# Splitting the slot copies of the first stage over two engines, and new places and queues in the tail of a two-layer convolution kernel

## The chip, the cores and the metric

The kernel runs on one core of a Trainium2 chip. The core has a matrix engine (PE), a vector engine (DVE), an activation engine (ACT), GpSimd (POOL) and a queue engine (SP), which share 16 DMA engines. The metric is the device time of one launch in microseconds (us). The kernel before took 1919.48 us, the median of three runs (1914.35, 1919.48, 1921.25).

## What is computed

The input `x` is an image of 512 x 512 positions with 64 channels in float32, 64 MiB. Two layers follow each other, each of the form `x = x + layer(group_norm(x))`, with 32 groups of two channels normalised over the whole image.

```python
def _L0_conv_ref(x, ...):
    xn = _ln(x, norm_w, norm_b)
    left, right = xn @ left_w + left_b, xn @ right_w + right_b
    m = sequence_mask.astype(xn.dtype)
    mask = (m[:, :, None] * m[:, None, :])[..., None]
    left  = left  * mask * sigmoid(xn @ lgate_w + lgate_b)
    right = right * mask * sigmoid(xn @ rgate_w + rgate_b)
    out = einsum('bkjd,bkid->bijd', left, right)
    out = _ln(out, onorm_w, onorm_b) @ out_w + out_b
    return out * sigmoid(xn @ ogate_w + ogate_b)

def _L1_conv_ref(x, w_real, w_imag):      # keeps 12 x 12 Fourier modes
    x_ft = fft2(x)[..., :12, :12]
    out_ft = einsum('bcmn,comn->bomn', x_ft, w_real + 1j * w_imag)
    return real(ifft2(zero_pad(out_ft)))
```

The mask zeroes the rows and columns whose mask bit is 0. The kernel uses that only about half of the rows and columns count.

## The kernel before

A branch at the end of the program takes `compact` when at most 256 rows (`K`) have a mask bit. The trace shows that this branch runs. It works in stages.

**First stage (lines 642 to 674).** Each row of the image has a rank, with the masked-in rows first. The image is cut into 16 column blocks (`NJ`) of 32 columns (`JC`). Four gathers per block (`gather`, POOL's indirect DMAs of 1 MiB) bring rows in the order of rank, 128 rows each: `r = 0, 1` go into the two halves of an `xg` tile, `r = 2, 3` into two `yg` tiles. PE transposes each quarter into PSUM (`x_ps`, line 664), and DVE takes mean and variance from there (`bn_stats`, line 665, 16 per block; every fourth block `join_chunks` joins them; after block 8 `make_weights` prepares the projection weights). Of `xg`, which holds the masked-in rows, every column is also copied into the big tile `xc`, at a slot that is read from memory: `slots_of` loads ranks into registers, 16 per load (line 634), and line 669 issues one ACT copy of 128 x 128 numbers for each of the 32 columns. A masked-out column goes to a dummy slot, so several copies can have the same target. `xg` has 3 buffers, `yg` has 2. The order of the work on each queue is the order of the program (`manual_schedule`): on POOL the four gathers of a block, on ACT two register loads and 32 copies per block. When the stage is over, `group_norm_affine` forms the affine of the norm, and the next stage transposes `xc` (line 690) and scales it on ACT (line 692).

**Middle stages (lines 677 to 839).** Projections and gates, the products over the rows for each of 64 channels, and their results in the tile `places`, 128 partitions with eight places of 64 x 64 numbers each. The change doesn't touch these stages.

**Output stage (lines 841 to 1116).** A software pipeline over steps `s`, eight to a unit, 32 units of 64 positions x 128 rows. A unit is gathered again from `x`, normalised and gated; `gated` multiplies (line 962) and `added` adds to x (line 966) in quarters (`c`), both on POOL, except the last quarter of the last unit, which `engine_of` sends to DVE. `store` writes the new image to `x1_h` from SP's queue, `transform` (line 982) multiplies a unit into the Fourier sums, `save` copies them to the tile `f_t` (pool `of`, two buffers) and writes them to `modes_d`, `statistics` (line 1000) takes the statistics for the second group norm on DVE, and `fetch(h)` reads modes back to `modes_t`, a part of place 7. `fetch(3)`, the last, is issued on ACT's queue.

**Tail (lines 1118 to 1245).** The pools `lx` (three tiles) and `lq` (all small tiles of the second layer) take the memory of the closed pools of the output stage, in this order. POOL clears `picks` (line 1135), `fetch(3)` follows, then POOL gathers the first 13 (`AHEAD`) row blocks of 1 MiB ahead into free parts of `places` and the `lx` tiles. PE and DVE meanwhile end the group norm, mix the modes (line 1167) and transform back. Then for each of 64 row blocks PE makes the correction (`l_ps`, line 1229), DVE adds it to the gathered x (line 1236), SP stores the result, and POOL gathers a block 13 ahead.

Of the kernel before, what the change touches and what calls it, by code (L numbers as in the profile page):

```python
# [17 lines left out]
P = 128  # L18
# [12 lines left out]
NJ = N // JC  # L31
K = 2 * P
AHEAD = 13
QB = 4


# [9 lines left out]
def conv_preact_kernel(ctx: ExitStack, tc: tile.TileContext, t: dict):  # L46
# [89 lines left out]
    def load_weights(pool, queue):  # L136


        def per_channel(name):
            v = pool.tile([P, 1], F32, name="v_" + name)  # L140
            for r in range(2):
                queue.dma_start(v[r * C : (r + 1) * C, :], t[name].rearrange("(c o) -> c o", o=1))
            return v

        norms = {name: (per_channel(name + "_w"), per_channel(name + "_b")) for name in ("norm", "onorm")}
        loaded = []

        for name, norm, parts, split in (
            ("sides", "norm", ("left", "right"), True),
            ("gates", "norm", ("lgate", "rgate"), True),  # L150
            ("ogate", "norm", ("ogate", "ogate"), False),
            ("out", "onorm", ("out", "out"), False),
        ):
            raw = pool.tile([P, P], F32, name="raw_" + name)
            b = pool.tile([P, 1], F32, name="v_" + name)
            if not split:
                nc.vector.memset(raw, 0.0)
            for r in range(2):
                for k in range(2):
                    if split or r == k:  # L160
                        queue.dma_start(raw[r * C : (r + 1) * C, k * C : (k + 1) * C], t[parts[k] + "_w"])
                queue.dma_start(b[r * C : (r + 1) * C, :], t[parts[r] + "_b"].rearrange("(c o) -> c o", o=1))
            loaded.append((name, *norms[norm], raw, b, C if split else P))

        def make(keep):

            with tc.tile_pool(name="wps", bufs=2, space=PSUM) as wps:
                for name, nw, nb, raw, b, k in loaded:
                    scaled = pool.tile([P, P], F32, name="scaled_" + name, tag="scaled")
                    nc.vector.tensor_scalar(scaled, raw, nw, None, ALU.mult)  # L170
                    ps = wps.tile([P, P + 1], F32, name="ps_" + name, tag="ps")
                    nc.tensor.matmul(ps[:, :P], center, scaled, start=True, stop=True)
                    nc.tensor.matmul(ps[:, P : P + 1], raw[:k], nb[:k], start=True, stop=True)
                    weights[name] = keep.tile([P, P], F32, name="w_" + name)
                    biases[name] = keep.tile([P, 1], F32, name="b_" + name)
                    nc.vector.tensor_copy(weights[name], ps[:, :P])
                    nc.vector.tensor_add(biases[name], ps[:, P : P + 1], b)

        return make
# [430 lines left out]
    def compact(fc):  # L610
# [14 lines left out]
        def gather(dst, src, idx, r, jc):  # L625
            nc.gpsimd.indirect_dma_start(  # L626
                out=dst, out_offset=None, in_=src, in_offset=bass.IndirectOffsetOnAxis(ap=idx[:, r, jc : jc + 1], axis=0)
            )

        def slots_of(engine, jc):  # L630

            regs = []
            for k in range(0, JC, 16):
                _, some = nc.values_load_multi_w_load_instructions(
                    slot_row[0:1, jc * JC + k : jc * JC + k + 16], engines=(engine,), min_val=0, max_val=K,
                    skip_runtime_bounds_check_because="a rank is not negative, and the minimum with K was taken",
                )
                regs += some
            return regs


        with tc.tile_pool(name="xc", bufs=1) as cp:
            xc = cp.tile([P, K + 1, 2, C], F32, name="xc")
            with tc.tile_pool(name="f1", bufs=1) as sp, tc.tile_pool(name="f1x", bufs=3) as xp, tc.tile_pool(
                name="f1y", bufs=2
            ) as yp, tc.tile_pool(name="f1p", bufs=6, space=PSUM) as pt, tc.manual_schedule():
                make_weights = load_weights(sp, nc.sync)
                sets = chunk_sets(fc, 4, 1)
                quarter = NJ // 4
                for jc in range(NJ):  # L650
                    if jc % quarter == 0:
                        stats = sp.tile([P, 1, 16 * quarter, 6], F32, name="stats1c")
                    xg = xp.tile([P, 2, JC, C], F32, name="xg")
                    of_row = [xg[:, 0], xg[:, 1]] + [yp.tile([P, JC, C], F32, name="yg") for _ in range(2)]
                    for r in range(4):
                        gather(of_row[r].rearrange("p j c -> p (j c)"), tiles, src_i, r, jc)
                    for r in range(4):
                        flat = of_row[r].rearrange("p j c -> p (j c)")
                        for c in range(4):

                            ps = pt.tile([P, 4, P], F32, name="x_ps")
                            for i in range(4):
                                o = (8 * c + 2 * i) * C
                                nc.tensor.transpose(ps[:, i, :], flat[:, o : o + P], ident)  # L664
                            nc.vector.bn_stats(  # L665
                                stats[:, 0, 16 * (jc % quarter) + 4 * r + c, :], ps.rearrange("p i k -> p (i k)")
                            )
                    for j, slot in enumerate(slots_of(mybir.EngineType.Activation, jc)):
                        nc.scalar.copy(xc[:, bass.ds(slot, 1)].rearrange("p o r c -> p (o r) c"), xg[:, :, j, :])  # L669
                    if jc % quarter == quarter - 1:  # L670
                        join_chunks(sp, sets, jc // quarter, stats)
                    if jc == NJ // 2:
                        make_weights(fc)
                ab1 = group_norm_affine(fc, sets, 2 * stats.shape[2], "xc")


# [113 lines left out]
        with tc.tile_pool(name="tri", bufs=1) as trp:  # L790
# [54 lines left out]

            units = [(jc, half) for jc in range(NJ) for half in ((1, 0) if jc < NJ - 1 else (0, 1))]
            total_g = (first + len(units)) * SIZE
            with tc.manual_schedule(), tc.tile_pool(name="late", bufs=1) as lp, tc.tile_pool(name="of", bufs=2) as fp:
                sets = chunk_sets(lp, 8)
                col_basis = lp.tile([P, 4, M2], F32, name="col_basis")  # L850
                nc.scalar.dma_start(col_basis, t["c_table"][:, :, 2:])
# [22 lines left out]

                def fetch(h):

                    (nc.scalar if h == 3 else nc.sync).dma_start(modes_t, modes_d[h * P : (h + 1) * P])

                with tc.tile_pool(name="np_x", bufs=LEAD + 2) as tp, tc.tile_pool(name="np_q", bufs=2) as sqp, tc.tile_pool(
                    name="np_s", bufs=3  # L880
# [67 lines left out]
                        for j, slot in enumerate(slots_of(mybir.EngineType.SP, jc)):  # L948
                            nc.sync.dma_start(us[jc][:, j], u_d[:, bass.ds(slot, 1)].rearrange("p o r c -> p (o r) c"))


                    def engine_of(k, c):
                        return nc.vector if (k, c) == (len(units) - 1, 3) else nc.gpsimd

                    def gated(k, c):

                        jc, half = units[k]
                        if half == 0:
                            u = us[jc][:, 16 * (c % 2) : 16 * (c % 2) + 16, c // 2, :]
                        else:  # L960
                            u = rows_of["out"].unsqueeze(1).to_broadcast([P, 16, C])
                        engine_of(k, c).tensor_mul(zs[k, c], zs[k, c], u)  # L962

                    def added(k, c):
                        xr = x_of(k)[:, 16 * c : 16 * c + 16, :]
                        engine_of(k, c).tensor_add(xr, xr, zs.pop((k, c)))  # L966

                    def store(k, r):
                        jc, half = units[k]
# [16 lines left out]
                            )  # L986

                    def save(jc):
                        ft = fp.tile([P, 8, C], F32, name="f_t")
                        nc.scalar.copy(ft.rearrange("p j c -> p (j c)"), fs.pop(jc))  # L990
                        for g in range(4):
                            o = jc * JC + 8 * g
                            queue = nc.scalar if jc == NJ - 1 else nc.sync
                            queue.dma_start(modes_d[o : o + 8].rearrange("j m c -> m j c"), ft[32 * g : 32 * g + M2])
# [29 lines left out]
                    for s in range(-LEAD, total_g + 2 * SIZE):  # L1024
# [3 lines left out]
                        def held(i):  # L1028
                            return 0 <= v - i < len(units)
# [24 lines left out]

                        if n % 2 == 1:
                            i, c = (0, (n - 3) // 2) if n >= 3 else (1, 3)
                            if held(i):
                                gated(v - i, c)
                        else:
                            i, c = (0, (n - 4) // 2) if n >= 4 else (1, 2 + n // 2)  # L1060
                            if held(i):
                                added(v - i, c)
                        if 0 <= v + 3 < len(units):
                            if n == 3:
# [50 lines left out]
                            for part, name in enumerate(("w_real", "w_imag")):  # L1115
                                nc.sync.dma_start(wide[part * C : (part + 1) * C], t[name].rearrange("c o m n -> c o (m n)"))

                with tc.tile_pool(name="lx", bufs=1) as xp, tc.tile_pool(name="lq", bufs=1) as qp:

                    free = 3 * 64 * C + C * MODES * MODES  # L1120
                    buffers = [places[:, free : free + JC * C].rearrange("p (n c) -> p n c", c=C)]
# [195 lines left out]
```

## Time and profile before

| what | us |
|---|---|
| median of the runs | 1919.48 |
| profiled execution, its own time | 1910.37 |
| its span | 1908.6 |
| first stage, first gather to first transpose of the next stage | 14.40 to 226.11 |
| output stage and join, up to the last bn_stats of line 1000 | to 1574.57 |
| tail, first gather ahead to the end of the span | 1582.18 to 1908.6 |

The mean granted clock of the matrix engine is 0.892 of full speed. Over the whole span PE is busy 88%, DVE 77%, ACT 51%, POOL 43%. These shares are averages over stages with different limits, so the slices and windows of a stage say more than the totals: the row of digits in the page has 40 slices of 47.7 us, of which the first five hold the first stage and the last seven the tail. A group's row gives line, engine, operation, output and input with shapes, count, busy time and mean of one in ns, and then the idle time of the engine just before those instructions with what ended it. An engine's idle time matters only where something waits for it.

### The profile page before, as it was taken

Reading aid. Unit: us, or ns where it says so; the run is one execution under the profiler, and the core shown is the slowest. Engines: PE = TensorE matmul, PEld = TensorE weight load, DVE = VectorE, ACT = ScalarE, POOL = GpSimd, SP = SyncE. Lnnn points to the kernel's source line nnn. Section 1 sums busy time; section 2 is a strip of 40 time slices with the busy share of each in tenths; the row PEclk is TensorE's granted clock in tenths of the full one; section 3 lists DMA queues with packets and bytes.
Section 4 is the critical chain, followed back from the end, with each engine's and each line's share of the span. In section 5 each row is a group of like instructions: output and inputs, shape, how many; then the busy total and the mean of one; then the engine's idle time right before and its main releaser. Section 6 shows DMA issues by size and latency. Waiting matters only on the chain. (4 is left out here: it accounts for less than half of the span.)

```text
span 1908.6 us, 33697 instructions
## 1 busy us (share of the span) xinstructions
PE 1672.8 (88%) x11598; PEld 1351.7 (71%) x11598; DVE 1462.3 (77%) x2995; ACT 971.5 (51%) x1766; POOL 825.9 (43%) x517
## 2 busy tenths in 40 slices
PE   6776499999899999999999899999999966987873
PEld 5666466665677889998888888888888835654431
DVE  6988477777455558888999799989999994764552
ACT  3777766564222254567777577767777720111000
POOL 2322011111000000019999799979998973111110
PEclk9998799999899999999999899999999986555555
DMA  7988235556655534236876576767777579999999
GB/s 266 415 334 332 85 100 138 139 136 153 205 177 177 177 128 160 120 120 238 277 250 240 213 246 229 249 224 242 267 259 252 199 218 360 404 427 427 426 427 380
DMA packets 188867, 468.21 MB, mean 245 GB/s; under 512 B 35184, under 2 KB 134384, under 8 KB 147600
## 3 DMA queue, kind: packets, MB, share of 16 engines
q1 hardware_dynamic: 158192, 262.40, 40.6%
q0 software_dynamic: 27712, 201.40, 27.4%
q10 hardware_dynamic: 2784, 2.16, 0.4%
q8 instruction: 94, 1.54, 0.3%
q14 instruction: 85, 0.70, 0.1%
HBM read 278.13 MB, written 187.76 MB: 244 GB/s over the span
## 5 line engine op out<-in xcount | busy, mean ns | idle before, releaser
L918 PE MATMUL w_ps<-gate_x,xt_c 128*128 128x128 f32 x2048 | 283.3, 282 | 31.5 <-DVE z_t L1087 30.0
L966 POOL TENSOR_TENSOR places<-places,z_t 128x1024 f32<-128x1024 f32 x127 | 301.7, 2376 | 8.2
L918 PEld LDWEIGHTS w_ps<-gate_x,xt_c 128*128 128x128 f32 x2048 | 254.4, 195 | 48.1 <-DVE z_t L1087 48.0
L918 PE MATMUL c_ps<-center_x,xt_c 128*128 128x128 f32 x2048 | 277.2, 279 | 0.0
L918 PEld LDWEIGHTS c_ps<-center_x,xt_c 128*128 128x128 f32 x2048 | 253.6, 195 | 2.2 <-ACT xt_c L913 1.8
L928 ACT ACTIVATE sq_c<-c_ps 128x512 f32<-128x512 f32 x320 | 188.8, 590 | 104.1 <-PE c_ps L918 103.7
L1229 PE MATMUL l_ps<-places,rinv 24*128 24x512 f32 x512 | 209.9, 1098 | 35.5 <-DVE places L1236 29.4
L1087 DVE TENSOR_TENSOR z_t<-w_ps,rs_n 128x512 f32<-128x512 f32 x320 | 216.7, 677 | 23.3 <-PE w_ps L918 22.9
L1000 DVE BATCH_NORM_STATS2 stats2c<-places 128x6 f32<-128x128 f32 x1024 | 220.8, 280 | 8.4 <-POOL places L966 8.4
L1045 ACT ACTIVATE z_t<-z_t 128x1024 f32<-128x1024 f32 x128 | 135.6, 1060 | 141.8 <-DVE z_t L1090 136.9
L932 DVE TENSOR_REDUCE scratch<-sq_c 128x16 f32<-128x1024 f32 x160 | 194.8, 1218 | 16.9 <-ACT sq_c L928 12.2
L1229 PEld LDWEIGHTS l_ps<-places,rinv 24*128 24x128 f32 x512 | 118.5, 296 | 121.6 <-DVE places L1236 80.0
L1090 DVE TENSOR_TENSOR z_t<-z_t,scratch 128x1024 f32<-128x1024 f32 x160 | 195.4, 1221 | 11.8 <-ACT rs_n L938 3.5
L962 POOL TENSOR_TENSOR z_t<-z_t,bias_row_out 128x1024 f32<-128x1024 f32 x63 | 149.7, 2376 | 113.0 <-DMA places<-u_d 108.7
L908 PE MATMUL t_ps<-c_ident,places 128*128 128x128 f32 x1280 | 197.0, 277 | 1.3 <-DVE places L837 1.3
L1236 DVE TENSOR_TENSOR places<-places,l_ps 128x512 f32<-128x512 f32 x200 | 125.0, 683 | 90.0 <-DMA places<-x_h,dst_i 60.6
L913 ACT ACTIVATE xt_c<-t_ps,ab_xc 128x512 f32<-128x512 f32 x256 | 175.9, 687 | 23.4 <-PE t_ps L908 23.3
L908 PEld LDWEIGHTS t_ps<-c_ident,places 128*128 128x128 f32 x1280 | 149.3, 143 | 51.7 <-issue 50.8
L626 POOL DMA_INDIRECT places<-in_x,src_i x64 | 62.8, 981 | 264.4 <-PE c_ps L918 213.1
L669 ACT COPY xc<-xg 128x128 f32 x512 | 153.3, 299 | 46.2 <-issue 30.5
L665 DVE BATCH_NORM_STATS2 stats1c<-x_ps 128x6 f32<-128x512 f32 x256 | 157.4, 690 | 14.3 <-PE x_ps L664 13.6
L962 POOL TENSOR_TENSOR z_t<-z_t,places 128x1024 f32<-128x1024 f32 x64 | 151.7, 2370 | 31.2 <-ACT z_t L1045 30.1
(201 smaller groups left out, 2551.8 us busy)
## 6 DMA issues: line engine op xcount, KB each, us to landing
x_h<-places SPq DMA_DIRECT2D x64, 1024.0 KB
out_x<-places SPq DMA_DIRECT2D x50, 1024.0 KB
places<-u_d SPq DMA_DIRECT2D x512, 64.0 KB
left_d<-o_c SPq DMA_DIRECT2D x64, 256.0 KB
right_d<-o_c SPq DMA_DIRECT2D x64, 256.0 KB
left_raw<-left_d SPq DMA_DIRECT2D x64, 256.0 KB
right_raw<-right_d SPq DMA_DIRECT2D x64, 256.0 KB
u_d<-z_t SPq DMA_DIRECT2D x32, 512.0 KB
```

What stands on the lines that cost most here:

```text
L665: nc.vector.bn_stats(stats[:, 0, 16 * (jc % quarter) + 4 * r + c, :], ps.rearrange("p i k -> p (i k)"))
L908: nc.tensor.transpose(tps[:, i, :], flat[:, o : o + P], ident)
L913: nc.scalar.activation(xts[s], tps, AF.Identity, bias=ab1[:, 2:3])
L918: nc.tensor.matmul(ps[:, 2 * i : 2 * i + 2, :], xts[s][:, i, :], w, start=True, stop=True)
L928: nc.scalar.activation(sqs[s // 2][:, 8 * (n % 2) : 8 * (n % 2) + 8, :], cps, AF.Square)
L932: nc.vector.tensor_reduce(totals[k % 2][:, 8 * (n - 1) : 8 * (n + 1)], sqs.pop(s // 2), AX.X, ALU.add)
L962: engine_of(k, c).tensor_mul(zs[k, c], zs[k, c], u)
L966: engine_of(k, c).tensor_add(xr, xr, zs.pop((k, c)))
L1000: nc.vector.bn_stats(st[k // 4][:, g, k % 4, :], x_of(k)[:, :, 2 * g : 2 * g + 2])
L1087: nc.vector.tensor_mul(z[:, 8 * odd : 8 * odd + 8, :], wps, rs)
L1090: nc.vector.tensor_add(z, z, bias.unsqueeze(1).to_broadcast([P, 16, C]))
L1229: nc.tensor.matmul(ps.rearrange("p j o -> p (j o)"), rinv[h, b, :], it[h], start=True, stop=True, tile_position=(32 * g, 0),)
```

## The change

There are two parts. In the first stage, `slots_of` takes a range of columns. A new helper `keep` issues the copies of a range on a given engine: columns 0 to 21 (`SHARE`) on ACT, 22 to 31 on POOL. Gathers are issued by a new helper `fetch_tile`, two blocks at the start and then block `jc + 2` after the copies of block `jc`; `xg` has 2 buffers, `yg` has 4. Two weight tiles are allocated in the pool of `xc`.

In the tail, the pool `of` is gone and `save` uses a part of place 7. `fetch(3)` is issued on POOL's queue. The last quarter of the last unit is done by `finished` on DVE, in two halves through two PSUM tiles, where the bias also lies in PSUM, and the add follows at once instead of one step later. The pools `lq` and `lx` are opened in the other order.

```diff
+SHARE = 22
...
-        def slots_of(engine, jc):
+        def slots_of(engine, jc, first=0, last=JC):
...
-            with tc.tile_pool(name="f1", bufs=1) as sp, tc.tile_pool(name="f1x", bufs=3) as xp, tc.tile_pool(
-                name="f1y", bufs=2
+            with tc.tile_pool(name="f1", bufs=1) as sp, tc.tile_pool(name="f1x", bufs=2) as xp, tc.tile_pool(
+                name="f1y", bufs=4
...
+                def fetch_tile(jc):
+                    xg = xp.tile([P, 2, JC, C], F32, name="xg")
+                    xgs[jc] = xg, [xg[:, 0], xg[:, 1]] + [yp.tile([P, JC, C], F32, name="yg") for _ in range(2)]
+                    for r, part in enumerate(xgs[jc][1]):
+                        gather(part.rearrange("p j c -> p (j c)"), tiles, src_i, r, jc)
+
+                def keep(engine, copy, jc, first, last):
+
+                    for j, slot in enumerate(slots_of(engine, jc, first, last), first):
+                        copy(xc[:, bass.ds(slot, 1)].rearrange("p o r c -> p (o r) c"), xgs[jc][0][:, :, j, :])
+
+                fetch_tile(0)
+                fetch_tile(1)
...
-                    for j, slot in enumerate(slots_of(mybir.EngineType.Activation, jc)):
-                        nc.scalar.copy(xc[:, bass.ds(slot, 1)].rearrange("p o r c -> p (o r) c"), xg[:, :, j, :])
+                    keep(mybir.EngineType.Activation, nc.scalar.copy, jc, 0, SHARE)
+                    keep(mybir.EngineType.Pool, nc.gpsimd.tensor_copy, jc, SHARE, JC)
+                    del xgs[jc]
+                    if jc + 2 < NJ:
+                        fetch_tile(jc + 2)
...
-                        make_weights(fc)
+                        make_weights(fc, cp)
...
-                    (nc.scalar if h == 3 else nc.sync).dma_start(modes_t, modes_d[h * P : (h + 1) * P])
+                    (nc.gpsimd if h == 3 else nc.sync).dma_start(modes_t, modes_d[h * P : (h + 1) * P])
...
+                    def finished():
+
+                        z = zs.pop((last, 3))
+                        made = [ps_c.tile([P, 8, C], F32, name="c_ps") for _ in range(2)]
+                        for i, ps in enumerate(made):
+                            u = bias_ps["out"].unsqueeze(1).to_broadcast([P, 8, C])
+                            nc.vector.tensor_mul(ps, z[:, 8 * i : 8 * i + 8, :], u)
+                        for i, ps in enumerate(made):
+                            xr = x_of(last)[:, 48 + 8 * i : 56 + 8 * i, :]
+                            nc.vector.tensor_add(xr, xr, ps)
...
-                        ft = fp.tile([P, 8, C], F32, name="f_t")
+                        ft = places[:, 7 * 64 * C + M2 * C : 7 * 64 * C + 32 * C].rearrange("p (j c) -> p j c", c=C)
...
-                with tc.tile_pool(name="lx", bufs=1) as xp, tc.tile_pool(name="lq", bufs=1) as qp:
+                with tc.tile_pool(name="lq", bufs=1) as qp, tc.tile_pool(name="lx", bufs=1) as xp:
```

More of the change, by code (lines that the diff above doesn't have):

```diff
@@ L163, in load_weights, with make @@
             loaded.append((name, *norms[norm], raw, b, C if split else P))
-        def make(keep):
+        def make(keep, slots=None):
             with tc.tile_pool(name="wps", bufs=2, space=PSUM) as wps:
@@ L173, in make @@
                     nc.tensor.matmul(ps[:, P : P + 1], raw[:k], nb[:k], start=True, stop=True)
-                    weights[name] = keep.tile([P, P], F32, name="w_" + name)
+                    home = slots if slots is not None and name in ("sides", "gates") else keep
+                    weights[name] = home.tile([P, P], F32, name="w_" + name)
                     biases[name] = keep.tile([P, 1], F32, name="b_" + name)
@@ L628, in gather @@
             )
-        def slots_of(engine, jc):
+        def slots_of(engine, jc, first=0, last=JC):
             regs = []
-            for k in range(0, JC, 16):
+            for k in range(first, last, 16):
                 _, some = nc.values_load_multi_w_load_instructions(
-                    slot_row[0:1, jc * JC + k : jc * JC + k + 16], engines=(engine,), min_val=0, max_val=K,
+                    slot_row[0:1, jc * JC + k : jc * JC + min(k + 16, last)], engines=(engine,), min_val=0, max_val=K,
                     skip_runtime_bounds_check_because="a rank is not negative, and the minimum with K was taken",
@@ L649, in compact @@
                 quarter = NJ // 4
+                xgs = {}
+                def fetch_tile(jc):
[8 more added lines that the diff above has]
+                fetch_tile(1)
                 for jc in range(NJ):
@@ L652, in compact @@
                         stats = sp.tile([P, 1, 16 * quarter, 6], F32, name="stats1c")
-                    xg = xp.tile([P, 2, JC, C], F32, name="xg")
-                    of_row = [xg[:, 0], xg[:, 1]] + [yp.tile([P, JC, C], F32, name="yg") for _ in range(2)]
                     for r in range(4):
-                        gather(of_row[r].rearrange("p j c -> p (j c)"), tiles, src_i, r, jc)
-                    for r in range(4):
-                        flat = of_row[r].rearrange("p j c -> p (j c)")
+                        flat = xgs[jc][1][r].rearrange("p j c -> p (j c)")
                         for c in range(4):
@@ L847, in compact @@
             total_g = (first + len(units)) * SIZE
-            with tc.manual_schedule(), tc.tile_pool(name="late", bufs=1) as lp, tc.tile_pool(name="of", bufs=2) as fp:
+            with tc.manual_schedule(), tc.tile_pool(name="late", bufs=1) as lp:
                 sets = chunk_sets(lp, 8)
@@ L949, in load_u @@
                             nc.sync.dma_start(us[jc][:, j], u_d[:, bass.ds(slot, 1)].rearrange("p o r c -> p (o r) c"))
-                    def engine_of(k, c):
-                        return nc.vector if (k, c) == (len(units) - 1, 3) else nc.gpsimd
                     def gated(k, c):
@@ L961, in gated @@
                             u = rows_of["out"].unsqueeze(1).to_broadcast([P, 16, C])
-                        engine_of(k, c).tensor_mul(zs[k, c], zs[k, c], u)
+                        nc.gpsimd.tensor_mul(zs[k, c], zs[k, c], u)
                     def added(k, c):
                         xr = x_of(k)[:, 16 * c : 16 * c + 16, :]
-                        engine_of(k, c).tensor_add(xr, xr, zs.pop((k, c)))
+                        nc.gpsimd.tensor_add(xr, xr, zs.pop((k, c)))
+                    def finished():
[7 more added lines that the diff above has]
+                            nc.vector.tensor_add(xr, xr, ps)
                     def store(k, r):
@@ L1056, in compact @@
                             i, c = (0, (n - 3) // 2) if n >= 3 else (1, 3)
-                            if held(i):
+                            if held(i) and (v - i, c) != (last, 3):
                                 gated(v - i, c)
+                            elif held(i):
+                                finished()
                         else:
                             i, c = (0, (n - 4) // 2) if n >= 4 else (1, 2 + n // 2)
-                            if held(i):
+                            if held(i) and (v - i, c) != (last, 3):
                                 added(v - i, c)
```

## The prediction

> **What bounds the kernel now.** I read the slices first, then the waits of 20 to 206 us, then the timeline around the end of the first stage and around the join before the tail.
>
> ```profile
> DVE  6988477777455558888999799989999994764552
> ACT  3777766564222254567777577767777720111000
> ```
>
> Wrong view for a verdict: no engine is full in the slices of the first stage (DVE 6, 9, 8, 8; ACT 3, 7, 7, 7). The windows and rows say more:
>
> ```profile
> 26.00:66.00 40.00, 30.74 (x252) 27.62 (x251) 37.81 (x63) 30.79 (x103) 13.71 (x15) 1.00 1.02 414
> 106.00:156.00 50.00, 36.21 (x272) 32.05 (x272) 42.83 (x83) 37.97 (x128) 15.03 (x16) 0.93 0.90 335
> POOL xg L626 <- ACT xc L669: 50.4, 11, 7.9
> ACT xc L669 <- issue: 28.5, 14, 2.1
> L669 ACT COPY xc<-xg 128x128 f32 x512 | 153.3, 299 | 46.2 <-issue 30.5
> L634 ACTq TENSOR_LOAD <-slot_row x32: 1006/1018/1035, 21.1 to 214.3; - x32
> 202.94 10.55 ACT L669 COPY xc<-xg 128x128 f32 x32 [2.04 <-issue]
> 215.51 10.54 ACT L669 COPY xc<-xg 128x128 f32 x32 [2.02 <-issue]
> 226.11 1.97 PE L690 MATMUL xc_ps<-c_ident,xc 128*128 128x128 f32 x8 [16.28 <-ACT xc L669]
> ```
>
> ACT has 38 busy us of 50, yet it is never free: between two blocks of 32 copies lie exactly 2.0 us, the two register loads of 1.02 us, which do not count as busy. A block costs 10.57 + 2.04 = 12.6 us, and 16 of them from 26.5 give 228; the last copy ends at 226.1. Until about 100 us the stock in the three buffers hides this (414 GB/s, DVE full); then POOL's gathers wait for ACT and the DMA falls to 335. At the end statistics are done at 206, and PE waits 16 us for copies. So **ACT bounds the first stage.** The middle stages are untouched; I move them rigidly. The tail is bound by DMA (427 GB/s to the end) once the gathers ahead run; its start:
>
> ```profile
> 1562.32 3.39 DVE L962 TENSOR_TENSOR z_t<-z_t,bias_row_out 128x1024 f32<-128x1024 f32 x1 [0.40 <-ACT z_t L1045]
> 1566.41 1.21 DVE L966 TENSOR_TENSOR places<-places,z_t 128x1024 f32<-128x1024 f32 x1
> 1570.26 1.98 ACTq L994 DMA_DIRECT2D modes_d<-f_t  x4
> 1576.42 0.35 ACTq L877 DMA_DIRECT2D places<-modes_d  x1
> 1578.09 3.94 POOL L1135 MEMSET picks<- 128x4608 f32 x1 [13.46 <-DVE set_var L1018]
> 1582.18 0.99 POOL L626 DMA_INDIRECT places<-x_h,dst_i  x1 [0.15 <-issue]
> ```
>
> POOL stands idle for 13.5 us for memory, not for data, while the DMA moves only 141 GB/s (1570 to 1580).
>
> **First stage, the copies.** ACT keeps 22: 22 x 0.330 (10.57/32) = 7.27, plus still two loads (16 and 6) 2.04 = 9.3 us a block. POOL gets per block one load (1.0), 10 copies, and has its four gathers at 0.94 + 0.30 gap = 5.0. A POOL copy of 128 numbers with an address from a register isn't in the trace. The nearest rows:
>
> ```profile
> L716 POOL COPY rbc<-rq_out 128x512 f32<-128x512 f32 x64 | 38.4, 616 | 238.1 <-DVE rq_out L207 170.0 <-PE rc_ps L722 37.5 <-PE xc_ps L690 21.3
> L1135 POOL MEMSET picks<- 128x4608 f32 x1 | 3.9, 3938 | 13.5 <-DVE set_var L1018 13.5
> ```
>
> 3938/4608 = 0.855 ns an element; 616 less 512 x 0.855 leaves 178 ns fixed; so 109 + 178 = **0.29 us**. Ends: 0.20 (fixed part hidden behind the one before), 0.62 (no cheaper than four times the size). The Trainium skill speaks against the move: GPSIMD Engine Reference, "Performance versus the Vector engine", calls the engine the wrong choice for ordinary elementwise work and gives 4497 ns for 2048 elements of a two-input add. At that rate (2.2 ns) plus the 178 ns it is 0.46 us. A copy reads one input, so I stay with the row; both sums are below.
>
> **Order between the engines.** Masked-out columns share a slot and addresses are known only at run time. Probably each engine's copies wait for the other's: ACT block, POOL block, next ACT block. Then a block costs 7.27 + 10 x 0.29 + about 0.3 for two handovers = 10.5 us, the loads hidden in the other engine's share; without it, ACT 9.3 and POOL 5.0 + 1.0 + 2.9 = 8.9 side by side.
>
> **What is late next.** DVE: 64 bn_stats took 38.56 us in the full stretch from 66.85, 0.6025 each, so 256 cost 154; three joins before the last block's end at 2.0, the weights after block 8 (117.5 to 124.8) about 7: from 22.6 that is 190. DMA: 67.1 MB at 414 GB/s = 162 us from 16, so 178, plus the last block's statistics. The weights stood in ACT's shadow and now count, since that cover is gone. I laid the blocks out one after another with these rows (gather 1.24 on POOL, 2.5 a MiB on the DMA after 0.94 + 2.2; the next gather of a buffer after both copies; POOL's fourth gather after PE's last transpose of the block before, and POOL's copies queued behind it). Statistics end at 190 to 193, copies at 182 (no order) to 192 (order), and the next stage's first scaling, 6.1 us after the statistics as now (205.97 to the affine at 211.9), at 196 to 199. It is at 227.31 now. At 0.46 us a copy with the order: 211 to 213 instead. **I take 199: -28 us.**
>
> **Buffers.** Two xg for three: a gather for block jc + 2 needs both engines' copies of jc, so one block is always under way. Lead by the layout: issued some 16 us before use, landed in 8 (median 8.0 now). Cost 0; if the cover went, 2.8 us a block (landing 5.3 at least less 2.5 transfer).
>
> **Tail, last quarter.** The DVE multiply took 3.39 beside a POOL add (1562.29 to 1564.63), the add 1.21 alone. With one operand in PSUM DVE isn't slowed beside POOL: 0.677 for line 1087, 128x512. Four of these, 2.7, end at 1565.0 instead of 1567.6; the 40 bn_stats that stood between and behind keep their 7.9: statistics end at 1572.9 instead of 1574.6. -1.7 us for the PE chain. Ends: -2.4 to 0.
>
> **Tail, memory and queues.** `picks` and `rinv` both wait for the last DVE instruction of the old pools, at 1577.95. With `lq` first it lies over the transposed tiles, last read by PE around 1557: memset at 1564.7 to 1568.6. Then `fetch(3)` blocks POOL until the modes are written: PE's sums end at 1568.5 (two halves of 1.92 from 1564.68), ACT copy 0.59, four issues 1.98, so 1571.2, landing about 3 later (3.4 in the row of u_d): 1574. Issue 0.6, gathers from **1575 instead of 1582**. Queued behind `fetch(3)` are the 13 gathers; ACT is freed of it, which changes nothing. The modes land near 1579 to 1580 (u_d's 3.4 plus 0.79 MB at 420 GB/s), the chain wants them at 1580.5. `lx` tiles now wait for the old pools, but their gathers are eleventh to thirteenth. `save` with one place: writes lie some 40 us apart, cost 0.
>
> DMA starts 7 earlier, but its 13 MiB and 2.4 MB of tables take 38 us, to 1613, and the first store (1615.87 now) can go at 1614.2: the queue runs dry for 3 to 4 us. Before, gathers reached to 1620 and never did. 115 transfers of 1 MiB follow either way. So **-4.5 us**, ends -8 and +1.
>
> **Sum.** -28 - 4.5 = -32.5: 1910.4 becomes 1878 as profiled. The median of the runs is 9 us above that execution, so 1919.5 - 32.5 = **1887**.
>
> **Rivals.**
> - POOL copies near the two-input price, ordered: next stage at 212, -15, tail -4.5: 1900. For it the register address; against it one read stream. 0.14.
> - Tail gives nothing, because modes land late or the dry queue eats it: 1891.5. For it the 1 us of slack. 0.12.
> - Two buffers starve the DMA: 2.8 us for 14 blocks = 39 takes the 28 and more than the tail: 1919 to 1926. For it, POOL's gathers wait behind its own copies; against, the layout's lead. 0.05.
> - Slower: POOL copies that cost as much as 512 elements, 0.62, in order with ACT's: 7.27 + 6.2 + 0.3 = 13.8 a block against 12.6, +19, less tail: 1934. It decides from (12.6 - 7.6)/10 = 0.50 us a copy. Against: the row's 0.855 ns an element. 0.05.
> - As forecast: 0.64, own range 1879 to 1895.
>
> The range 1873 to 1905 runs from 0.2 us copies without order and -8 in the tail to the dear copies, with the 5 us by which runs differ. A change below 0.5% (9.6 us) can't be told from none. Faster 0.88, same 0.06, slower 0.06.
>
> **What would show it.** ACT's blocks of 22 copies of 7.3 us, at starts 10 to 10.5 apart; POOL copies near 0.29; DMA near 414 GB/s to the end of the stage; DVE full to about 192; scaling at line 692 near 199. Gaps of ACT longer than 2 us that end with POOL mean the order. In the tail DVE's four operations at 0.68, memset at 1565 less the shift, first gather ahead 7 us earlier, a short dip of DMA before the first store. I am wrong if POOL's copies pass 0.4 us or the DMA rate stays at 335.

## The result, and the profile after

The changed kernel takes 1890.0 us, the median of four runs (1885.77 to 1893.94), against 1917.34 (1914.35 to 1921.25) for the kernel before, also four runs. The ratio is 0.9856, with a 95% interval of 0.9822 to 0.989. The predicted time was 1887, the predicted own range 1879 to 1895.

The profiled execution took 1886.98 us (span 1885.2, mean granted clock 0.893), 23.4 less than the profiled one of before. By stages it divides so:

| stretch, us | before | after | difference | predicted |
|---|---|---|---|---|
| start to the first scaling of the next stage | 227.31 | 209.64 | -17.7 | -28 |
| from there to the multiply of the last quarter | 1335.0 | 1334.4 | -0.6 | 0 |
| from there to the end of the span | 346.3 | 341.2 | -5.1 | -4.5 |

The middle row, whose code is nearly the same in all kernels here (only the place to which `save` copies differs), took between 1327.5 and 1343.5 us in the runs below. So a total from one run says little about an edit worth 5 us. The stages, each measured from its own start, say more, and the verdicts below rest on them.

First the slices of the changed kernel, which answer to those shown of before:

```profile
DVE  5989677777555568888999799979999994665552
ACT  3565555653222255567777677757767720111000
```

ACT fell from 7 to 5 or 6 in slices 2 to 4, and DVE reads 5, 9, 8, 9 at the start where it read 6, 9, 8, 8. As before, no slice names what bounds the stage. Two of its windows (window, length, busy us of PE, PEld, DVE, ACT and POOL, then clock, DMA share and GB/s):

```profile
26.00:66.00 40.00, 28.93 (x227) 26.05 (x226) 33.44 (x55) 26.54 (x88) 20.11 (x42) 0.96 0.99 377
106.00:156.00 50.00, 41.38 (x280) 33.48 (x280) 42.73 (x82) 29.97 (x102) 28.68 (x58) 0.90 0.96 375
```

Its waits from 20 to 206 us (engine and line that waited, what it waited for, us in total, times, longest):

```profile
POOL xc L663 <- ACT xc L663: 46.5, 15, 8.6
ACT xc L663 <- POOL xc L663: 39.5, 11, 3.6
ACT xc L663 <- DMA xg<-in_x,src_i: 17.5, 4, 5.4
```

The groups of copies in the same stretch (busy us, mean ns of one, idle time before):

```profile
L663 ACT COPY xc<-xg 128x128 f32 x352 | 105.0, 298 | 67.9 <-POOL xc L663 39.5 <-DMA xg<-in_x,src_i 17.5
L663 POOL COPY xc<-xg 128x128 f32 x160 | 46.9, 293 | 56.9 <-ACT xc L663 46.5 <-issue 1.4
```

And POOL's register loads (ns shortest, median, longest):

```profile
L636 POOLq TENSOR_LOAD <-slot_row x16: 2267/2280/2293, 21.9 to 192.0; - x16
```

The two engines wait for each other, ACT 39.5 us and POOL 46.5. The end of the stage in the timeline (start, us, then the instructions, with the idle time before them and its releaser):

```profile
181.50 7.23 ACT L663 COPY xc<-xg 128x128 f32 x22 [3.58 <-POOL xc L663]
188.80 3.54 POOL L663 COPY xc<-xg 128x128 f32 x10 [2.21 <-ACT xc L663]
192.37 7.23 ACT L663 COPY xc<-xg 128x128 f32 x22 [3.64 <-POOL xc L663]
199.66 3.49 POOL L663 COPY xc<-xg 128x128 f32 x10 [7.32 <-ACT xc L663]
209.64 1.45 ACT L708 ACTIVATE gc_t<-xc_ps,ab_xc 128x512 f32<-128x512 f32 x2 [10.04 <-DVE ab_xc L276]
```

The second engine never copies at the same time as the first. A block takes 7.23 + 3.5 and the small handovers, 10.82 us from one ACT block to the next (181.50 to 192.37 is 10.87), where it took 12.6. POOL's copies come one every 0.35 us, ACT's every 0.33, so 32 copies cost as much as they did on ACT alone. What is gone is the time in which nobody copied: the two register loads of 1.02 us each. They now run in the other engine's turn, and so does POOL's own load of 2.28 us: in 15 of the 16 blocks POOL's first copy starts 0.06 or 0.07 us after ACT's last (188.73 to 188.80 above), so it waited for ACT and not for its load.

In the tail, the timeline around the last quarter:

```profile
1544.01 1.29 DVE L986 TENSOR_TENSOR c_ps<-z_t,scratch 128x512 f32<-128x512 f32 x2 [0.40 <-ACT z_t L1068]
1546.27 3.94 POOL L1160 MEMSET picks<- 128x4608 f32 x1
1549.16 1.97 ACTq L1017 DMA_DIRECT2D modes_d<-places  x4
1552.78 0.59 POOL L893 DMA_DIRECT2D places<-modes_d  x1 [2.56 <-DMA modes_d<-places]
1553.67 1.00 POOL L628 DMA_INDIRECT places<-x_h,dst_i  x1 [0.30 <-issue]
```

The idle 13.5 us of POOL before the memset are gone. The windows around the first store (at 1594.63):

```profile
1585.00:1590.00 5.00, 3.32 (x16) 3.09 (x16) 2.29 (x3) 1.92 (x3) 0.00 (x0) 0.66 1.02 419
1590.00:1595.00 5.00, 3.27 (x14) 2.13 (x16) 2.92 (x6) 0.91 (x1) 0.00 (x0) 0.78 0.46 193
1595.00:1600.00 5.00, 5.00 (x17) 3.37 (x15) 4.63 (x8) 0.00 (x0) 0.73 (x1) 0.50 0.88 362
```

The DMA runs dry just before the first store (a share of 0.46, then 0.88). Before, with the first store at 1615.87, it did not:

```profile
1610.00:1615.00 5.00, 3.14 (x17) 1.60 (x16) 2.66 (x4) 1.52 (x2) 0.00 (x0) 0.84 1.01 421
```

### The profile page after: what moved, and what is told of

It reads as the page before. It is cut to its first block, busy times and chain, and to the rows that moved or that the text cites. A ratio compares the mean times of both kernels' runs of the same rounds, so it can differ in the third digit from the quotient of the medians.

```text
span 1885.2 us, 33737 instructions
## 1 busy us (share of the span) xinstructions
PE 1683.2 (89%) x11598; PEld 1350.9 (72%) x11598; DVE 1458.5 (77%) x2997; ACT 922.0 (49%) x1606; POOL 873.0 (46%) x678
## 5 line engine op out<-in xcount | busy, mean ns | idle before, releaser
L1115 DVE TENSOR_TENSOR z_t<-z_t,scratch 128x1024 f32<-128x1024 f32 x160 | 195.4, 1221 | 11.7 <-ACT rs_n L954 3.4
L628 POOL DMA_INDIRECT places<-in_x,src_i x64 | 62.6, 978 | 261.9 <-PE c_ps L934 210.9
L678 DVE BATCH_NORM_STATS2 stats1c<-x_ps 128x6 f32<-128x512 f32 x256 | 156.0, 683 | 12.2 <-PE x_ps L677 11.3
L853 DVE SCALAR_TENSOR_TENSOR places<-tri_c_ps,slot_t,mask_s 128x256 f32<-128x256 f32 x128 | 73.1, 650 | 85.3 <-PE tri_c_ps L849 85.3
```

Source lines behind the costliest of these rows:

```text
L678: nc.vector.bn_stats(stats[:, 0, 16 * (jc % quarter) + 4 * r + c, :], ps.rearrange("p i k -> p (i k)"))
L1115: nc.vector.tensor_add(z, z, bias.unsqueeze(1).to_broadcast([P, 16, C]))
```

## Experiments

Two theories stood at the start. **Turns**: the engines copy in turn, and the gain is the hidden register loads alone. **Sides**: the engines copy side by side, and what limits the stage is data, statistics or the buffers. For the tail the question was which of its edits carries the 5 us. "Tail" below is the time from the multiply of the last quarter to the end of the span: 341.2 in the changed kernel, and between 340.8 and 342.6 in the five runs e1, e2, e3, e4 and e9, whose tail code is the same.

**e1_no_order and e9_no_order_even: no order between the two engines.** POOL's copies go to a tile of their own, ACT's to slots in plain order. Both runs leave the sorting of the columns out, so only their times are of use.

```diff
-            xc = cp.tile([P, K + 1, 2, C], F32, name="xc")
+            xc = cp.tile([P, K, 2, C], F32, name="xc")
+            aside = cp.tile([P, 1, 2, C], F32, name="aside")
...
-                    keep(mybir.EngineType.Pool, nc.gpsimd.tensor_copy, jc, SHARE, JC)
+                    keep(mybir.EngineType.Pool, nc.gpsimd.tensor_copy, jc, SHARE, JC, aside, few_row, 0)
```

> POOL's copies go to a small tile of their own and ACT's to slots in plain order (both leave the sorting of the columns out), so that the two engines no longer write one tile; number, size and register addresses of the copies stay. Theory 'turns' (ACT and POOL copies wait for each other): ACT's blocks of 22 come 9.3 us apart at first (10.8 with the order) and then follow the data at about 10; POOL's copies keep 0.35 us each; first scaling of the next stage (gc_t) at 196 to 201 instead of 209.6. Rival 'two buffers' (the loop of gather, landing and copies with two xg buffers sets the pace): pitch stays at 10.8, gc_t at 207 or later.

The first scaling came at 205.77, 3.9 before the changed kernel's. Both kinds of waits between ACT and POOL are gone, yet ACT still stood idle. Its blocks in the timeline of e1:

```profile
111.07 7.23 ACT L667 COPY xc<-xg 128x128 f32 x22 [1.81 <-issue]
123.15 7.28 ACT L667 COPY xc<-xg 128x128 f32 x22 [4.85 <-issue]
132.25 7.23 ACT L667 COPY xc<-xg 128x128 f32 x22 [1.82 <-issue]
```

Its register loads on ACT:

```profile
L639 ACTq TENSOR_LOAD <-slot_row x32: 755/1337/3522, 19.5 to 190.9; - x32
```

The gaps alternate between 1.8 and 4.8, and the loads of registers take up to 3.5 us (0.75 to 1.04 in the changed kernel). The edit let a block start at slot 22 x `jc` (from block 11 on at 234). The gap is 1.8 where that is a multiple of 4, as at slots 44 and 88, and 4.8 where it is only even. The edit had put a cost of its own in the place of the one that it removed, so it was repeated with starts at 16 x `jc`, which are all multiples of 4:

```diff
-            at = min(SHARE * jc, K - SHARE) if last == SHARE else jc * JC
+            at = 16 * jc if last == SHARE else jc * JC
```

> As e1_no_order, but ACT's register loads start at multiples of 16 slots, as in the changed kernel: in e1 every second gap of ACT was 4.8 us instead of 1.8, with register loads of up to 3.5 us. Theory 'turns': ACT's blocks now come 9.1 us apart until they wait for data, then as the data come, about 10; no gap of 4.8; copies end before the statistics, statistics at 191 to 197, gc_t 6 us behind them: 197 to 203 instead of 209.6. Rival 'two buffers': blocks 10.8 apart also now, gc_t at 206 or later.

The first scaling came at 200.78, 8.9 before the changed kernel's. The largest sum of waits of ACT in e9:

```profile
ACT xc L667 <- DMA xg<-in_x,src_i: 45.3, 15, 5.7
```

Its first two windows:

```profile
26.00:66.00 40.00, 29.82 (x248) 26.71 (x247) 37.55 (x62) 26.94 (x89) 23.55 (x52) 1.00 1.02 411
66.00:106.00 40.00, 30.92 (x258) 27.60 (x257) 39.86 (x71) 26.26 (x88) 26.85 (x57) 1.00 1.01 419
```

Blocks near its end in the timeline:

```profile
160.74 7.23 ACT L667 COPY xc<-xg 128x128 f32 x22 [2.71 <-DMA xg<-in_x,src_i]
164.10 3.52 POOL L667 COPY aside<-xg 128x128 f32<-128x128 f32 x10
170.67 7.24 ACT L667 COPY xc<-xg 128x128 f32 x22 [2.70 <-DMA xg<-in_x,src_i]
```

Now the copies overlap (160.74 to 167.97 and 164.10 to 167.62), and DMA and DVE are as full early on as before the change (411 GB/s, 37.55 of 40). The turns are shown: their price is 8.9 us in this pair of runs, and between 4.6 and 10 beside all runs with the changed first stage (205.34 to 210.89). A block still takes 10 us, not the 9.3 that the prediction gave ACT without the order. ACT now waits for data, and the DMA has no more to give: its share from 66 to 106 is 1.01, and a block's 4 MiB at 419 GB/s take 10.0 us.

The edit removed one thing more than the order. POOL's slot is always 0 now, and e9 has no register load on POOL, where the changed kernel has 16 of 2.28 us. What is left on its line is

```profile
L639 POOLq EVENT_SEMAPHORE  x16: 17/17/17, 22.1 to 176.9; - x16
```

The order with these loads gone, or the loads kept and the order gone, was not run. But in the changed kernel the loads held up POOL's copies in one block only (by 1.4 us), so they hardly account for the 8.9.

**e2_act_all: the split undone, the new buffers and gather order kept.**

```diff
-SHARE = 22
+SHARE = 32
...
-                    keep(mybir.EngineType.Pool, nc.gpsimd.tensor_copy, jc, SHARE, JC)
```

> Split undone, new buffers and gather order kept: ACT does all 32 columns. Theory 'turns': pitch 10.57 + 2.04 = 12.6 us, as in the kernel before, gc_t at 226 to 230: buffers and gather order give nothing by themselves. Rival: part of the gain comes from the buffers and the two blocks under way; then gc_t at 215 or earlier.

The first scaling came at 226.95 (227.31 before), and blocks are 12.58 apart. Buffers and gather order by themselves bring nothing and cost nothing.

**e3_share27: 27 columns for ACT, 5 for POOL.** The edit is `SHARE = 27`.

> 27 columns on ACT, 5 on POOL. Theory 'turns': a block costs 27 x 0.329 and then the longer of POOL's 5 x 0.349 + 0.1 = 1.85 and ACT's two loads, 2.04: 10.9 us, so nearly nothing changes (10.82 with 22): gc_t at 209 to 213. If POOL's share took work off ACT, moving five columns back would cost 5 x 0.329 = 1.6 us a block, 26 us in all: gc_t at 225 or later.

It came at 210.86 (209.64 with 22), and the total was 1892.26. POOL's five copies take 1.72 and its load 1.18 us, and a block takes 11.12 to 11.17: 27 x 0.329 = 8.88, plus ACT's two loads (1.01 and 1.24), which POOL's shorter turn no longer covers. Copies cost nearly the same on either engine, so the ratio matters only until a turn gets shorter than the other engine's loads. By itself the run doesn't tell the theories apart: ACT's own chain would be 11.1 us side by side, too. What it shows is that the share is no lever.

**e4_weights2: the weights prepared after block 2 instead of 8.**

```diff
-                    if jc == NJ // 2:
+                    if jc == 2:
                         make_weights(fc, cp)
```

> The projection weights are made after block 2 instead of after block 8. Theory 'bare weights' (the 8 us in which PE and DVE make the weights lie on the path, since DVE is full behind them and starved before them): statistics end at 196 to 199 instead of 203.4; the copies' chain still ends at 203, gc_t at 204.5 to 206.5, 3 to 5 us earlier. Rival: only the copies' chain counts and DVE would have waited anyway: gc_t stays at 209 to 210.

It came at 205.22, as expected: -4.4. But this verdict did not last. e10_ahead14 below has the first stage of the changed kernel without any edit, and came at 205.34; there, ACT waited 11.7 us for data in 3 waits (17.5 in 4 in the changed kernel). With weights after block 8 the changed kernel, e5, e6, e7, e8 and e10 gave 209.64, 209.14, 209.89, 209.88, 210.89 and 205.34; after block 2, e4 and e11 gave 205.22 and 205.5. That speaks for a gain but doesn't show it.

**e5_first_alone: only the first stage changed, the tail as before** (its lines of the diff taken back).

> First stage of the changed kernel, tail of the kernel before. Parts add up: gc_t at 209.6, all later work 17.7 us earlier, the tail's own length (multiply of the last quarter to the end of the span) 346.3 us as before; total 1917 - 18 = 1899. If the two parts help each other, the total lies above 1903.

1895.19 us (1892.43 to 1898.32, four runs) against 1913.4 (seven runs): ratio 0.9888 (0.9852 to 0.9924). The first scaling came at 209.14, and the tail took 348.0. So the first stage alone brings about 18 us in the total as well as in the profile.

**e6_tail_pools, e7_tail_fetch, e8_tail_last: one edit of the tail undone in each.**

```diff
-                with tc.tile_pool(name="lq", bufs=1) as qp, tc.tile_pool(name="lx", bufs=1) as xp:
+                with tc.tile_pool(name="lx", bufs=1) as xp, tc.tile_pool(name="lq", bufs=1) as qp:
```

> Changed kernel, but lx opened ahead of lq as before. Theory 'memory': the clearing of picks waits again for the last DVE instruction of the old pools, 15.7 us after the last quarter's multiply starts less the 2 us won there, so 13.5 to 14; first gather ahead at 18 us after that multiply instead of 9.7, DMA without the dip before the first store; multiply to end 344 to 346 us instead of 341.2. Rival 'queue' (the gain is from fetch(3) on POOL): 341 to 342.

```diff
-                    (nc.gpsimd if h == 3 else nc.sync).dma_start(modes_t, modes_d[h * P : (h + 1) * P])
+                    (nc.scalar if h == 3 else nc.sync).dma_start(modes_t, modes_d[h * P : (h + 1) * P])
```

> Changed kernel, fetch(3) back on ACT's queue. POOL isn't held for the modes' landing: gathers ahead start right after the clearing, about 6.3 us after the last quarter's multiply instead of 9.7; fetch(3) is issued behind the join at about 12, lands behind the gathers' traffic: columns' matmuls wait, first store 0 to 4 us later. By the theory that the first store sets the end once the gathers start early: multiply to end 341 to 345. Rival (start of the gathers sets the end): 338 to 339.

```diff
-                        nc.gpsimd.tensor_mul(zs[k, c], zs[k, c], u)
+                        (nc.vector if (k, c) == (last, 3) else nc.gpsimd).tensor_mul(zs[k, c], zs[k, c], u)
...
-                        nc.gpsimd.tensor_add(xr, xr, zs.pop((k, c)))
+                        (nc.vector if (k, c) == (last, 3) else nc.gpsimd).tensor_add(xr, xr, zs.pop((k, c)))
```

(and `finished` is no longer called)

> Changed kernel, last quarter again by two SBUF operations on DVE. Multiply takes 3.4 us beside POOL's add, statistics end 12.2 us after it starts instead of 10.2; modes written 2 us later, first gather at 11.5 to 12 instead of 9.7, first store 2 us later: multiply to end 343 instead of 341.2. Rival (hidden under DMA): 341.2.

Each event in us after the multiply of the last quarter; `t_ps` is the last multiply of the modes fetched last:

| | before | after | e6 pools | e7 fetch | e8 last | e5 none |
|---|---|---|---|---|---|---|
| statistics end | 12.2 | 10.2 | 10.2 | 10.2 | 12.3 | 12.3 |
| first gather ahead | 19.9 | 9.7 | 18.2 | 6.4 | 12.5 | 19.5 |
| `t_ps` starts | 19.9 | 17.5 | 21.9 | 21.5 | 19.5 | 19.5 |
| first store | 53.5 | 50.6 | 55.9 | 54.3 | 53.5 | 56.6 |
| end | 346.3 | 341.2 | 347.1 | 345.3 | 346.4 | 348.0 |
| end less first store | 292.8 | 290.6 | 291.2 | 291.0 | 292.9 | 291.4 |

Each single step back costs 4 to 6 us, and all three together bring no more than 5 to 7. The edits don't add up; they need one another. The last two rows say why: the end follows the first store (290.6 to 292.9 behind it), not the first gather. In e7 the gathers start 3.3 us earlier than in the changed kernel, and the end is 4.1 later. The timelines of e6 (first three lines) and e7 show what holds the store back:

```profile
1550.77 3.94 POOL L1160 MEMSET picks<- 128x4608 f32 x1 [11.04 <-DVE set_var L1041]
1554.65 0.60 POOL L893 DMA_DIRECT2D places<-modes_d  x1
1559.30 5.28 PE L888 MATMUL t_ps<-col_basis,places 128*128 128x24 f32 x24 [4.72 <-DMA places<-modes_d]
```

```profile
1554.77 1.96 ACTq L1017 DMA_DIRECT2D modes_d<-places  x4
1556.00 0.99 POOL L628 DMA_INDIRECT places<-x_h,dst_i  x1 [0.15 <-issue]
1561.46 0.54 ACT L1034 ACTIVATE stats2c<-stats2c 128x256 f32<-128x256 f32 x1 [6.72 <-DVE stats2c L225]
1561.63 0.35 ACTq L893 DMA_DIRECT2D places<-modes_d  x1
1571.14 5.29 PE L888 MATMUL t_ps<-col_basis,places 128*128 128x24 f32 x24 [4.32 <-DMA places<-modes_d]
```

In e6 `fetch(3)` stands on POOL behind a memset that again waits for the old pools, so the modes come later than in the changed kernel. In e7 two things happen. The fetch stands on ACT's queue behind a step of the statistics (line 1034), so that from the last issue of the write to the issue of the fetch are 4.9 us (1556.73 to 1561.63), where the changed kernel has 1.65 (1551.13 to 1552.78). The kernel before had 4.2 there without any gathers under way (1572.24 to 1576.42), so this part is the queue's.

And the modes land late: from the issue to `t_ps`, which waits for them, are 9.5 us, against 4.65 in e6, where the gathers are issued behind it. It isn't ACT's queue that makes the landing slow: in e5 the fetch stands there too, with no gathers under way, and `t_ps` started 5.4 us after its issue (1562.60 to 1568.00) without a wait for the modes. Without the gathers, then, the modes of e7 would have been there about 17 us after the multiply (an estimate: issue at 12.0, landing 4.65 to 5.4), not at 21.5. So the wait of POOL before `fetch(3)`, which looks like a loss, keeps the DMA free for the small transfers on the chain.

In the changed kernel, as in the one before, `t_ps` waits not for the modes but for DVE's statistics (`rq_v`); that is why the shorter last quarter counts there (e8). In e8, as before the change, another 2 us are lost after the first store; where is open.

**e10_ahead14: a 14th block gathered ahead,** into the half of place 7 in which the modes lay, once they have been read, to close the dip of the DMA.

```diff
-AHEAD = 13
+AHEAD = 14
...
-                    for jb in tiles_left[:AHEAD]:
+                    for jb in tiles_left[: AHEAD - 1]:
...
                         columns(3, tcp)
+                    fetch_rows(*tiles_left[AHEAD - 1])
```

> Changed kernel with one more row block gathered ahead in the tail (14), into the first half of place 7, after the modes have been read from there. Theory 'first store': the DMA's dip before the first store (3.7 us lost in the changed kernel) takes one more MiB, 2.46 us; first store as before at 50.6 to 51.3 after the last quarter's multiply, multiply to end 338.5 to 340 instead of 341.2 to 342.6. Rival (the later tail is bound by stores and PE, so gathers ahead are of no use): 341 or more.

The tail took 339.9, with 289.5 after the first store (290.6): about 1 us. e11, with the same edit, gave 340.0; both lie just below the range of the five runs without it (340.8 to 342.6).

**e11_best: e10 with the weights after block 2 and 26 columns on ACT.**

> 14 blocks ahead, weights after block 2, and 26 columns on ACT with 6 on POOL. First stage: copies end near 200, statistics 197 to 200, gc_t at 204 to 206 instead of 209.6; tail multiply to end 339 to 340. Together 6 to 7 us below the changed kernel: 0.982 of the kernel before where the changed one had 0.9856.

1883.45 us (1879.85 to 1889.28, six runs) against 1913.87 (eleven runs): ratio 0.9851 (0.9825 to 0.9877). In the profile the first scaling came at 205.5 and the tail took 340.0, 5 us less together than in the changed kernel; the totals, 0.9851 beside 0.9856, don't tell the two apart. The expected gain is a miss, and no version here is shown to beat the changed kernel.

## Why the prediction was right, and where it was off

**What bounds the stage: right.** ACT's chain of loads and copies did, not data: with the new buffers and ACT alone (e2) the stage kept its time.

**Copy on POOL: right.** 0.29 us was worked out, 0.293 measured. From 128 to 512 numbers a copy grows by 0.841 ns each ((616 - 293)/384), close to the 0.855 taken from the memset, so the working holds and not only its number. The dear copies of the first rival (0.46) and of the slower one (0.62) did not come. But the engine's time for one copy isn't its pitch: ten took 3.49, not 2.9.

**Order: right.** It was taken as probable; e9 shows it. A block is 10.82 rather than 10.5: 0.6 more for POOL's pitch, 0.2 less for handovers.

**POOL's register load: missed, at little cost.** 1.0 was put down, 2.28 measured. ACT's turn of 7.2 covers it in 15 of 16 blocks. In one it came late, behind a gather that waited for PE: ACT was done at 143.63, POOL's copies began at 145.00.

**The first stage, -28: the term that failed.** It gave -17.7, in e5 to e8 -16.4 to -18.2, in e10 -22. The sum had statistics end at 190 to 193 and copies at up to 192; they ended at 203.35, and at 199.6 (ACT) and 203.15 (POOL). The sum did not hold in itself: 16 blocks of 10.5 from 26.5 end at 194.5, not at 192. Three more sizes were off. The pitch: 15 x 0.32 = 4.8. Lost time beyond the turns: from the first block (26.7) to the last (192.37) are 165.7 us, 3.4 more than 15 x 10.82, of which 1.4 are POOL's late load and 2.0 waits of ACT for data. And DVE: the layout kept it fed, but data come at the pace of the turns, 377 GB/s in place of 414 from 26 to 66, where DVE had 33.44 busy us, not 37.81. It ran full only at the end and finished 10 us late. Even without the turns (e9) statistics end at 194.46, later than the 190 to 193 of the sum. The step from the statistics to the first scaling (6.1) held: 6.3.

**Buffers at cost 0: right within the turns.** e2 shows no loss, and the starved DMA of the third rival did not come. Waits for data of 2.0 us beyond the turns are left. It isn't settled whether a third buffer would have removed them; this was not tried.

**Tail: right in its sum, -5.1 for -4.5.** DVE's four operations end 2.5 us after their start (2.7 predicted), statistics end 2.0 earlier (1.7), and the dip cost the DMA about 3.5 us (3 to 4; 5 us each at 0.46 and 0.88 where 1.02 is full: 2.8 + 0.7). The gathers start 10.2 earlier, not 7. The prediction took `fetch(3)` on POOL as a wait, with the modes just in time; e7 shows that it is worth more as a barrier. That "tail gives nothing" was wrong too, and e6 to e8 show how near it was: with any one of the three edits missing it would have been right.

**The total** came 3 us from the prediction, and part of this is chance. By the profiled executions the change is worth 23.4, not 32.5; the medians differ by 27.3, since runs of one kernel lie 7 to 14 us apart.

## What to carry to other kernels

Two engines that write one tile at addresses known only at run time copied in turns here, not side by side. In such a case count on hiding what lies between the copies (here 2 us of register loads a block), and not on halving them. When a tail is bound by DMA after its first store, ask what sets that first store, and keep the small transfers on its chain ahead of the bulk ones, even if the bulk starts later. Several edits around one handover may be worth nothing one by one, so test each by taking it back from the whole, not only by adding it to the kernel before.

## What the hardware showed that was not expected

- The time of a register load depends on how many are loaded and on where the slice begins. On ACT, 16 registers took 1.02 us and 6 took 0.75 when the slice began at a multiple of 4 (in e1 also at slots 44 and 60, which are no multiples of 16); from other even slots they took 3.5 and 1.34. That is about 0.25 us for four registers in the first case and 0.22 for each one in the second (an estimate from these loads). POOL's loads all began at other slots, and cost about 0.23 for each register: 10 from slot 22 took 2.28, 5 from 27 took 1.18. A POOL load from a multiple of 4 was not run.
- A POOL copy of 128 x 128 numbers to a run-time address is busy for 0.293 us, but such copies come 0.35 apart.
- The first stage of one and the same code ended between 205.3 and 210.9 us in six profiles, apart by as much as the edits that were to be told apart by it.
